# Products of a constant on the unread PSUM columns of two delta-rule scans

## The chip, the cores and the metric

The kernel runs on one core of one Trainium2 chip, as one launch. The metric is the device time of that launch in microseconds. The kernel before took 4370.02 us, the median of three runs (4360.15 to 4377.07 us). One further execution was profiled; all views of the profile below are of it.

The names used for the engines are those of the profile: PE is TensorE (PEld its weight loads), DVE is VectorE, ACT is ScalarE, POOL is GpSimd, SP is SyncE.

## The reference, cut to what matters

The program is a network of eight stages (L0_attn, L0_ffn, L1_attn, L1_ffn, L2_attn, L2_ffn, L3_attn, L3_ffn) over an input of 8 sequences x 512 tokens x 128 features, in float32. The change touches two of them, L0_attn and L2_attn. Each holds a delta rule: a state matrix per head is corrected token by token, and each token reads it. In L2_attn it is gated:

```
def step(S, inp):
    q_t, k_t, v_t, g_t, b_t = inp
    S = S * jnp.exp(g_t)[..., None, None]
    kv = jnp.einsum('bhk,bhkv->bhv', k_t, S)
    delta = (v_t - kv) * b_t[..., None]
    S = S + k_t[..., :, None] * delta[..., None, :]
    o = jnp.einsum('bhk,bhkv->bhv', q_t, S)
    return (S, o)
```

L0_attn has the same rule without the decay, written over chunks of 32 tokens. Both have 4 heads with keys of 32; the values are 32 wide in L0_attn and 64 wide in L2_attn, so a state row over all heads has W = 128 columns in L0_attn and W = 256 in L2_attn.

## The kernel before

The kernel goes through the stages one after the other. Tokens lie on the 128 partitions; a sequence is 4 tiles of 128 tokens (TPB = 4).

**How a delta rule is computed.** The kernel takes a chunk of 128 tokens at a time. Inside a chunk the token-by-token recurrence becomes a triangular system, whose inverse is built ahead of the scan for all 16 (head, chunk) pairs of a sequence by `inverse_steps` (L1244): blocks of 32x32 first, by doubling, with 64 products of 32x32 for each half step (L1275 `px`, L1282 `pz`), then blocks of 64 (L1294 to L1328). `pair_scores` (L1376) makes the token-by-token products `ps_a` (L1387). The scan itself, `scan_steps` (L1331), then goes through the four chunks in order. For a chunk c it issues on PE

- `pk` (L1344): the keys times the state S, W columns; DVE adds it to the values (`dr`, L1346). Not for c = 0, where the state is zero;
- `pd` (L1351): four products, one for each head, of the inverse with `dr` (with the values for c = 0), dv columns each; ACT copies the result out (`dd`, L1353);
- `pS` (L1357): the keys times `dd`, W columns, the update of the state; DVE masks it (`dS`, L1359), then POOL (L1362) or DVE (L1364) adds the old state. Not for c = 3;
- `po` (L1365): the queries times the state (L1367) and four products with `dd` (L1370), the output, which the stage's own `out` takes from PSUM (L481 in L0_attn, L1562 in L2_attn).

That is 3 + 4 + 4 + 3 = 14 PSUM tiles for a sequence. Each tile is a whole bank, 128 x 512 float32, of which only the first W columns are written and read. They come from the ring `psD`, which has two banks in both stages (L263, L1403); `single` (L814) hands out the next one of the ring.

**What sets the order of the work around the scan.** Both stages run several sequences at different phases at once. `together` (L1608) takes generators and advances the one that is furthest behind its share of steps, so that scan steps of one sequence stand between inverse steps of the next, preparation of the one after, and output work of the one before (L267 to L277 in L0_attn, L1425 to L1432 in L2_attn). On top of that the tile framework places each engine's instructions itself when the program is built, so instructions that depend on nothing yet may come to stand elsewhere than in the text. Once built, each engine runs its list in order, and waits on semaphores of the others.

**Number formats.** All of the products named above have float32 operands. A product with float32 operands appears in the trace as two pairs of weight load and matmul; one with bfloat16 operands as one pair. L2_attn already has one product in bfloat16 for each chunk, which adds a mask by way of an identity: L1522, `pdec<-cm,id`, 512 columns, its moving operand repeated over the heads by a broadcast (`bc`, L22).

Of the kernel before, what the change touches and what calls it, by code (L numbers as in the profile page):

```python
# [10 lines left out]
BF16 = mybir.dt.bfloat16  # L11
# [4 lines left out]
P = 128  # L16
# [5 lines left out]
def bc(ap, axis, n):  # L22
    a = ap.unsqueeze(axis)
    shape = list(a.shape)
    shape[axis] = n
    return a.to_broadcast(shape)


class Net:
# [186 lines left out]
    def L0_attn(self):  # L216

        nc, tc, T, NB, NT = self.nc, self.tc, self.T, self.NB, self.NT  # L220
        H, E, NL = 4, 32, 2
        with ExitStack() as es:
            cp = es.enter_context(tc.tile_pool(name="a0", reuse_waits="tile", side="right", bufs=1))
            w = {k: self.load(cp, f"L0_attn_{k}_proj_w", [D, D]) for k in ("q", "k", "v", "o")}
            cw = {k: self.load(cp, f"L0_attn_{k}_conv_w", [D, 4]) for k in ("q", "k", "v")}
            w["b"] = self.load(cp, "L0_attn_b_proj_w", [D, H])
            fs = self.load(cp, "L0_attn_fir_short_w", [D, 5])
            bones = self.load(cp, "c_hmask32", [P, H])
            bd = self.load(cp, "c_bmask32", [P, P])
            hT = cp.tile([D, NB, L], F32, name="hT")  # L230

            vt = cp.tile([P, TPB + 1, NB, D], F32, name="vt")
            nc.gpsimd.memset(vt[:, 0], 0.0)
            ls = cp.tile([P, NB, TPB, D], F32, name="ls")
            ll = cp.tile([P, NT, D], F32, name="ll")
            gc = es.enter_context(tc.tile_pool(name="a0g", reuse_waits="tile", side="right", bufs=1))
            lp = es.enter_context(tc.tile_pool(name="a0l", reuse_waits="tile", bufs=1))
            self.inverse_buffers(gc, 1)
            f = {"w1a": self.load(gc, "fw1a", [D, D], src=T["L0_attn_fuse_w1"][:D, :])}

            f["w1b"] = gc.tile([P, D], F32, name="w1b")
            nc.vector.memset(f["w1b"], 0.0)
            for h in range(H):
                nc.sync.dma_start(f["w1b"][h * 32 : h * 32 + 16, :], T["L0_attn_fuse_w1"][D:, :])
            f["st"] = gc.tile([P, TPB, H, 32], F32, name="st")
            nc.gpsimd.memset(f["st"], 0.0)
            f["b1"] = self.load(gc, "L0_attn_fuse_b1", [D, 1])
            f["w2"] = gc.tile([D, 32], F32, name="w2")
            nc.gpsimd.memset(f["w2"], 0.0)
            nc.sync.dma_start(f["w2"][:, :4], T["L0_attn_fuse_w2"])  # L250
            f["b2"] = self.load_row(gc, "L0_attn_fuse_b2", 4)
            f["onw"] = self.load(gc, "L0_attn_o_norm_w", [D, 1])
            f["rs"] = [self.load_row(gc, f"L0_attn_res_scale_{k}", 1) for k in ("short", "long")]
            lt = self.load_row(gc, "L0_attn_logit_temp", 1)
            tm = gc.tile([P, 1], F32, name="tm")
            self.softplus(tm, lt, gc, [P, 1])
            nc.vector.tensor_scalar(tm, tm, 1e-4, None, ALU.add)
            nc.vector.reciprocal(tm, tm)
            f["tm"] = tm
            st = [{"b": b, "hT": hT[:, b, :], "vt": vt[:, 1:, b, :], "ls": ls[:, b], "ll": ll[:, b * TPB : (b + 1) * TPB, :]} for b in range(NB)]  # L260
            self.ps = es.enter_context(tc.tile_pool(name="ps", reuse_waits="tile", bufs=1, space=bass.MemoryType.PSUM))
            last = es.enter_context(tc.tile_pool(name="psl", reuse_waits="tile", side="right", bufs=1, space=bass.MemoryType.PSUM))
            self.rings = {"psA": 1, "psC": 1, "psD": 2, "psF": (2, last)}  # L263
            for b in range(NB):
                self.L0_values(hT[:, b, :], vt[:, 1:, b, :], ls[:, b], w["v"], cw["v"], fs, lp, b)
            fir = self.L0_fir(vt, ll, lp)
            for n in range(-1, NB + 2):  # L267
                part = lambda m, g, k, late=0.0: (g(st[m]), k, late) if 0 <= m < NB else None
                self.together(
                    part(n, lambda s: self.inverse_steps(s["NT"], lp, "psC"), 15),  # L270
                    part(n - 1, lambda s: self.L0_scan(s, bd, lp), 12),
                    part(n - 2, lambda s: self.L0_fuse(s, f, w["o"], lp), 14),
                    part(n + 1, lambda s: self.L0_prep(s, w, cw, bones, lp), 11),
                    (fir, 16) if n == -1 else None,

                    *((self.L0_route(b, lp), 4, b * 0.1) for b in range(NB - 1) if n == NB + 1),
                )  # L277
            for _ in self.L0_route(NB - 1, lp):
                pass
# [964 lines left out]
    def inverse_steps(self, NT, pool, tag):  # L1244
# [77 lines left out]
        for u in range(2):  # L1322
# [5 lines left out]
            nc.vector.tensor_copy(nt[:64, gs, 64:], grp(pz[:64, :], 64))  # L1328
            yield

    def scan_steps(self, dv, kbT, qT, NT, AT, vb, kt, bd, out, pool, tag, ac=None):  # L1331

        nc = self.nc
        H = 4
        W = H * dv
        S = None
        for c in range(TPB):
            cs = slice(c * P, (c + 1) * P)  # L1340
            r = vb[:, c, :]
            if S is not None:
                pk = self.single(tag, "pk")
                nc.tensor.matmul(pk[:, :W], kbT[:, cs], S, start=True, stop=True)  # L1344
                r = pool.tile([P, W], F32, tag="dr", name="dr", bufs=1)
                nc.vector.tensor_tensor(r, vb[:, c, :], pk[:, :W], ALU.add)  # L1346
                yield
            pd = self.single(tag, "pd")
            for h in range(H):
                hs = slice(h * dv, (h + 1) * dv)  # L1350
                nc.tensor.matmul(pd[:, hs], NT[:, h, c, :], r[:, hs], start=True, stop=True)  # L1351
            dl = pool.tile([P, W], F32, tag="dd", name="dd", bufs=2)
            nc.scalar.copy(dl, pd[:, :W])  # L1353
            yield
            if c < TPB - 1:
                pS = self.single(tag, "pS")
                nc.tensor.matmul(pS[:, :W], kt[:, c, :], dl, start=True, stop=True)  # L1357
                Sn = pool.tile([P, W], F32, tag="dS", name="dS", bufs=2)
                nc.vector.tensor_tensor(Sn, pS[:, :W], bd, ALU.mult)  # L1359
                if S is not None:  # L1360
                    if ac is None:
                        nc.gpsimd.tensor_tensor(Sn, Sn, S, ALU.add)  # L1362
                    else:
                        nc.vector.scalar_tensor_tensor(Sn, S, ac[:, c : c + 1], Sn, ALU.mult, ALU.add)  # L1364
            po = self.single(tag, "po")  # L1365
            if S is not None:
                nc.tensor.matmul(po[:, :W], qT[:, cs], S, start=True, stop=False)  # L1367
            for h in range(H):
                hs = slice(h * dv, (h + 1) * dv)
                nc.tensor.matmul(po[:, hs], AT[:, h, c, :], dl[:, hs], start=S is None, stop=S is None or h == H - 1)  # L1370
            out(c, po[:, :W])
            if c < TPB - 1:
                S = Sn
            yield
# [17 lines left out]
    def L2_attn(self):  # L1392
# [3 lines left out]
        nc, tc, T, NB = self.nc, self.tc, self.T, self.NB  # L1396
        H, V = 4, 64
        with ExitStack() as es:
            cp = es.enter_context(tc.tile_pool(name="a2", reuse_waits="tile", side="right", bufs=1))
# [16 lines left out]
            for k, src in (("id", "ident"), ("cm", "c_cmaskT")):  # L1416
                f = self.ident if src == "ident" else self.load(cp, src, [P, P])
                c[k] = cp.tile([P, P], BF16, name=f"{k}16")
                nc.vector.tensor_copy(c[k], f)
            na = cp.tile([P, H], F32, name="na")  # L1420
            nc.scalar.activation(na, row["A_log"], AF.Exp)
            nc.vector.tensor_scalar(na, na, -1.0, None, ALU.mult)
# [752 lines left out]
```

## Time and profile before

| | us |
|---|---|
| median of 3 runs | 4370.02 (4360.15 to 4377.07) |
| the profiled execution, its own time | 4375.92 |
| its span, first to last instruction | 4374.1 |
| PE busy in the span | 3713.5 (85%) |
| DVE busy | 2393.6 (55%) |
| ACT busy | 1691.1 (39%) |
| POOL busy | 1575.7 (36%) |
| mean granted TensorE clock | 0.822 of full speed |

The profiled execution took 5.9 us more than the median of the runs; 1.8 us of its time lie outside its span.

How to read it: "busy" is the time in which at least one instruction of the engine is under way. PE's instructions overlap, so a busy PE need not be a PE at its peak. The granted clock is that of TensorE alone, as a share of its full speed; the profile has it for each piece of the span. The scans run from 211 to about 740 us (L0_attn) and from 2449 to 2988 us (L2_attn).

### The profile page before, as it was taken

What the parts mean: (1) busy time and instruction counts of PE and PEld (TensorE: products, weight loads), DVE (VectorE), ACT (ScalarE), POOL (GpSimd) and SP (SyncE); (2) the same over time, 40 slices, a digit from 0 to 9 for tenths busy, and PEclk for the clock granted to TensorE, in tenths of its full rate; (3) what the DMA queues carried; (4) which work ended last, traced back from release to release, by engine and by line L of the source; (5) the groups of instructions that cost most, each with busy time, mean ns of one, the idle gap of its engine ahead of it and who ended that gap; (6) DMA issues with size and microseconds to landing.
All of it is one profiled execution on the core that took longest, in us unless ns stands there. A gap on an engine that the chain in (4) does not pass through costs nothing.

```text
span 4374.1 us, 101816 instructions
## 1 busy us (share of the span) xinstructions
PE 3713.5 (85%) x44392; PEld 2680.3 (61%) x44456; DVE 2393.6 (55%) x5943; ACT 1691.1 (39%) x2545; POOL 1575.7 (36%) x1557
## 2 busy tenths in 40 slices
PE   5999998648999999897376999996999899986998
PEld 3777786545655656554254777774666566655666
DVE  6446565335454454554627566534777776655333
ACT  3224333113444444443024445422556566631221
POOL 1212221462111111222274343423455555423775
PEclk6566656678999999997586778766999999997998
DMA  2200000240200000000140000001000000002554
GB/s 66 60 3 2 3 7 14 82 127 1 82 7 2 4 7 1 4 1 20 29 84 13 3 3 3 2 3 41 1 1 1 1 1 7 1 8 72 149 147 126
DMA packets 125917, 130.60 MB, mean 30 GB/s; under 512 B 18496, under 2 KB 107280, under 8 KB 125472
## 3 DMA queue, kind: packets, MB, share of 16 engines
q0 software_dynamic: 30816, 67.62, 5.9%
q1 hardware_dynamic: 94656, 56.47, 4.5%
q8 instruction: 349, 5.72, 0.5%
q14 instruction: 96, 0.79, 0.1%
HBM read 96.85 MB, written 27.20 MB: 28 GB/s over the span
## 4 chain that ended last, share of the span: by engine, by line
PE 44%; DVE 16%; ACT 7%; POOL 5%; DMA 4%; issue 3%; POOLq 0%; another core or an unknown queue 0%; DVEq 0%; ACTq 0%; SPq 0%
PE ps_h L1023 4%; PE po L1029 3%; DMA acc<-y,tl_idx 2%; PE ps_qk L1721 2%; PE ps_s L897 2%; POOL nm_r L70 2%; DVE nm_st L65 2%; DVE mt L906 2%; PE ps_a L1387 1%; PE ps_tr L825 1%; PE ps_s L975 1%; PE pav L965 1%; PE po L1837 1%; PE pg L1984 1%; POOL r L1751 1%
## 5 line engine op out<-in xcount | busy, mean ns | idle before, releaser
L70 POOL TENSOR_TENSOR nm_r<-nm_r,mhalf 128x4 f32<-128x4 f32 x168 | 173.3, 1032 | 448.9 <-DVE nm_r L69 430.7
L1733 POOL TENSOR_TENSOR r<-r,rot 128x512 f32<-128x512 f32 x128 | 162.8, 1272 | 305.3 <-DVE rot L1732 249.4
L1030 DVE TENSOR_TENSOR y<-y,po 128x512 f32<-128x512 f32 x32 | 22.0, 687 | 307.9 <-PE po L1029 307.9
L928 POOL TENSOR_TENSOR cn<-cx,rc 64x448 f32<-64x448 f32 x32 | 37.5, 1173 | 413.5 <-DVE rc L926 413.5
L1023 PE MATMUL ps_h<-hTm,w 128*128 128x512 f32 x256 | 162.0, 718 | 11.2 <-ACT hid L1024 4.8
L979 ACT ACTIVATE pT<-ps_s 128x2048 f32<-128x2048 f32 x64 | 106.5, 1664 | 167.7 <-PE ps_s L977 167.7
L1721 PE MATMUL ps_qk<-wqkv,hTq 128*128 128x512 f32 x256 | 148.1, 674 | 18.3 <-DVE hTq L1713 6.1
L1271 POOL TENSOR_TENSOR iM<-iN,c_lvl 128x512 f32<-128x512 f32 x64 | 86.7, 1365 | 183.2 <-PE px L1275 167.1
L975 PE MATMUL ps_s<-qa,kT 32*128 32x256 f32 (+1 forms) x1024 | 149.7, 405 | 0.6 <-DVE mt L906 0.3
L624 POOL DMA_INDIRECT xr<-rows_in,tl_idx x124 | 118.8, 958 | 71.4 <-PE pt L671 17.5
L621 POOL DMA_INDIRECT acc<-y,tl_idx x78 | 124.8, 1600 | 45.1 <-DVE y L1994 21.7
L1024 ACT ACTIVATE hid<-ps_h,b 128x512 f32<-128x512 f32 x128 | 87.9, 687 | 130.7 <-PE ps_h L1023 129.6
L1029 PEld LDWEIGHTS po<-w,hid 128*128 128x128 f32 x1024 | 121.7, 198 | 20.9 <-ACT hid L1024 20.9
L1029 PE MATMUL po<-w,hid 128*128 128x128 f32 x1024 | 127.8, 285 | 5.8 <-ACT hid L1024 1.6
L1751 POOL TENSOR_TENSOR r<-r,rn 128x512 f32<-128x512 f32 x128 | 129.0, 1041 | 1.9
L1282 PEld LDWEIGHTS pz<-iTT,iX 32*32 32x32 f32 x8192 | 92.5, 120 | 51.4 <-issue 33.7
L1282 PE MATMUL pz<-iTT,iX 32*32 32x32 f32 x8192 | 103.7, 208 | 23.3 <-issue 16.5
L1723 ACT ACTIVATE sq<-ps_qk 128x512 f32<-128x512 f32 x128 | 75.8, 592 | 122.1 <-PE ps_qk L1721 122.0
L1275 PEld LDWEIGHTS px<-iT,iM 32*32 32x32 f32 x8192 | 96.8, 125 | 41.3 <-issue 27.3
L906 DVE TENSOR_REDUCE mt<-ps_s 128x8 f32<-128x2048 f32 x32 | 73.4, 2292 | 87.2 <-PE ps_s L899 87.2
L1275 PE MATMUL px<-iT,iM 32*32 32x32 f32 x8192 | 107.5, 213 | 10.6 <-issue 9.3
L1789 DVE TENSOR_REDUCE mx<-ps_s 128x8 f32<-128x1024 f32 x64 | 77.8, 1216 | 61.9 <-PE ps_s L1786 61.9
(681 smaller groups left out, 10626.8 us busy)
## 6 DMA issues: line engine op xcount, KB each, us to landing
fcur<-in_L_attn_fir_cur SPq DMA_DIRECT2D x32, 256.0 KB, 2.8
acc<-z SPq DMA_DIRECT2D x16, 512.0 KB, 6.9
sum<-acc SPq DMA_DIRECT2D x32, 256.0 KB, 3.0
rows_out<-y SPq DMA_DIRECT2D x23, 128.0 KB, 2.9
x<-in_L_attn_hidden_states SPq DMA_DIRECT2D x8, 256.0 KB, 4.8
fprev<-in_L_attn_fir_prev SPq DMA_DIRECT2D x8, 256.0 KB, 3.6
rows_in<-rx SPq DMA_DIRECT2D x8, 256.0 KB, 2.3
w<-in_L_attn_W SPq DMA_DIRECT2D x8, 256.0 KB, 2.8
```

Of the source, the lines that this page charges most:

```text
L70: nc.gpsimd.tensor_tensor(r, r, self.mhalf[:, :G], ALU.pow)
L621: self.nc.gpsimd.indirect_dma_start(out=dst, out_offset=bass.IndirectOffsetOnAxis(ap=idx, axis=0), in_=src, in_offset=None, compute_op=ALU ...
L624: self.nc.gpsimd.indirect_dma_start(out=dst, out_offset=None, in_=src, in_offset=bass.IndirectOffsetOnAxis(ap=idx, axis=0))
L906: nc.vector.tensor_reduce(m4, s4, AX.X, ALU.max, negate=True)
L975: nc.tensor.matmul(ss[:, h, n * 256 : n * 256 + W], kT[R[h], k * P : (k + 1) * P], qa[R[h], k * P : k * P + W], start=True, stop=False)
L1023: nc.tensor.matmul(ps, self.cols(w["w1"], f), hT, start=True, stop=True)
L1029: nc.tensor.matmul(self.cols(po, t), self.cols(hid[:, f, :], t), w["w2"][:, f, :], start=(f == 0), stop=(f == FC - 1))
L1275: nc.tensor.matmul(px[p, g * B : (g + 1) * B], nm[p, g, :], Ti[p, g, :], start=True, stop=True)
L1282: nc.tensor.matmul(pz[p, g * B : (g + 1) * B], X[p, g, :], TT[p, g, :], start=True, stop=True)
L1721: nc.tensor.matmul(ps, self.cols(hT, t), w["qkv"][:, j, :], start=True, stop=True)
L1733: nc.gpsimd.tensor_tensor(r3, r3, m, ALU.add)
L1751: nc.gpsimd.tensor_tensor(r3, r3, bc(rn[:, j, t, :], 2, E), ALU.mult)
```

## The change

A constant `fill`, the identity in bfloat16, is made in each of the two stages. Each of the 14 PSUM tiles of a scan is now taken through a new function `busy`. It takes the bank from the ring as before, and then issues two products of `fill` with `fill` (repeated over the columns by a broadcast) into the columns W to 511 of that bank, which nobody reads: 384 columns in L0_attn, 256 in L2_attn. The scan's own products follow into the first W columns.

```
@@ L0_attn and L2_attn, each
+            self.fill = cp.tile([P, P], BF16, name="fill")
+            nc.vector.tensor_copy(self.fill, self.ident)
@@ new, ahead of scan_steps
+    def busy(self, tag, name, used):
+
+
+        ps = self.single(tag, name)
+        for _ in range(2):
+            self.nc.tensor.matmul(ps[:, used:], self.fill, bc(self.fill, 1, (512 - used) // P), start=True, stop=True)
+        return ps
+
@@ scan_steps
-                pk = self.single(tag, "pk")
+                pk = self.busy(tag, "pk", W)
...
-            pd = self.single(tag, "pd")
+            pd = self.busy(tag, "pd", W)
...
-                pS = self.single(tag, "pS")
+                pS = self.busy(tag, "pS", W)
...
-            po = self.single(tag, "po")
+            po = self.busy(tag, "po", W)
```

## The prediction

> **What bounds the kernel now.** I first read the page's slices of the span, each 109 us long: how busy PE is, and which TensorE clock was granted.
>
> ```profile
> PE   5999998648999999897376999996999899986998
> ...
> PEclk6566656678999999997586778766999999997998
> ```
>
> In both stages of the change (slices 2 to 7 and 23 to 27 of 40) PE is nearly always busy, yet its clock stands at 5 or 6 tenths in the first and 6 to 8 in the second, against 9 in most slices of the other stages. The view by stretches puts numbers on the two scans:
>
> ```profile
> core 0: us, PE busy (x) PEld busy (x) DVE busy (x) ACT busy (x) POOL busy (x), PEclk, DMA share, GB/s
> 200.00:745.00 545.00, 507.58 (x10352) 416.58 (x10351) 308.27 (x625) 191.71 (x313) 123.72 (x135) 0.60 0.02 5
> 2448.00:2985.00 537.00, 496.75 (x10483) 407.71 (x10481) 295.57 (x628) 228.90 (x350) 184.01 (x179) 0.75 0.01 3
> ```
>
> PE is busy for 93% of each stretch, DVE, the next, for 57% and 55%. So PE sets the end of both, and what a product costs there depends on the clock. The clock's own records hold two values alone, 0.5 and 1.0, for pieces that are multiples of 3.413 us; a mean of 0.60 is 33 such windows of 160 at full clock, 0.75 is 80 of 157. What opens it? I asked for single windows, cut where the records cut.
>
> ```profile
> 423.22:426.63 3.41, 3.41 (x136) 3.35 (x133) 0.48 (x2) 3.38 (x7) 1.27 (x1) 0.50 0.02 5
> 426.63:430.05 3.42, 3.42 (x135) 3.13 (x136) 2.75 (x10) 1.84 (x3) 0.00 (x0) 0.50 0.02 5
> ...
> 2539.47:2542.88 3.41, 3.41 (x10) 1.92 (x8) 0.42 (x1) 1.65 (x3) 1.27 (x1) 0.50 0.02 5
> 2542.88:2546.29 3.41, 3.41 (x141) 2.77 (x141) 1.26 (x2) 0.57 (x2) 0.00 (x0) 1.00 0.02 5
> ```
>
> The first three are all wholly busy at half clock; only after the third does the clock open. They differ in what the timeline of PE shows in them:
>
> ```profile
> 423.06 1.93 PE L1275 MATMUL px<-iT,iM 32*32 32x32 f32 x128
> 424.92 0.80 PE L1357 MATMUL pS<-dd,kt 128*128 128x128 f32 x2
> 425.51 1.75 PE L1370 MATMUL po<-dd,AT 128*128 128x32 f32 x8
> ...
> 2539.43 1.21 PE L1344 MATMUL pk<-dS,kbT 128*128 128x256 f32 x2
> 2540.44 0.63 PE L1522 MATMUL pdec<-cm,id 128*128 128x512 bf16 x1
> 2540.87 1.91 PE L1521 MATMUL pdec<-gm,c_gt 128*128 128x512 f32 x2
> ```
>
> So I counted columns. A column that streams past a full 128x128 float32 stationary counts 1, one past a smaller stationary a quarter, one of a bfloat16 product a half; an instruction is spread evenly over its duration. The first window holds about 1024 (128 x 32 / 4) + 256 (2 x 128) + 150 = 1430, the third about 510 + 256 + 1024 + 140 = 1930. Counted so over all 1275 windows of the trace, the next window is at full clock after 5 of the 444 below 1500, after 9 of the 26 from 1500 to 1550, and after 804 of the 805 above, whichever clock they had themselves. I take 1547 as the mark, where a fit puts it. The quarter is fitted too (0.25). The half is the weak weight: few windows at the mark hold bfloat16, and 0.45 to 0.8 fit about equally well; 0.3 misjudges 28 windows in place of 12.
>
> The Trainium skill, "TensorE: Matmul & The Clock Gate", section "Why this matters for your kernels", speaks against the change: it asks only that TensorE be kept busy for 4 us or more and have no idle gaps. By it, windows like the first two, PE busy without a gap, should be at full clock already, and more work could only cost; the sum would be that of the slower rival below. The windows decide against the rule here: busy at 0.50 is their usual state.
>
> **The change, part by part.** Each sequence takes 14 banks through `busy`, with two products each: 14 x 2 x 8 = 224 in each stage, as many matmuls and weight loads as the built program shows more on PE. Nothing is removed. One DVE cast a stage (the like of L1419, 0.22 us) falls into the stages' preparation, where DVE is about half idle; uncovered it is 0.4 us in all.
>
> *Price of one product.* L1522 is the same form: bfloat16, an identity, 512 columns, broadcast. Its durations contain latency, so I take end to end. At half clock it ends 2540.44 + 0.63 = 2541.07, L1344 ahead of it 2540.64: 0.43 us (0.426 in the records' nanoseconds). At full clock:
>
> ```profile
> 2461.95 0.70 PE L1344 MATMUL pk<-dS,kbT 128*128 128x256 f32 x2
> 2462.48 0.38 PE L1522 MATMUL pdec<-cm,id 128*128 128x512 bf16 x1
> ```
>
> 2462.86 - 2462.65 = 0.21 (0.216). Scaled by columns, 384 cost 0.320 or 0.162 us, 256 cost 0.213 or 0.108. They lie on the path: PE's idle time is 7% of the stretches, and mostly elsewhere.
>
> *Weight loads.* The first product of a scan tile ended 0.51 us after a 32x32 product (L1357 after L1275, half clock, median of 7) but 0.21 us after a full-array one: its load had been exposed by 0.30 (0.20 at full clock). About 100 of the 224 tiles come after a small product. A fill in between hides that load in the two thirds of tiles where the built order leaves it directly ahead, and exposes its own load (0.15 or 0.10, L1522's): 100 x (2/3 x 0.25 - 0.125) = 4 us gained, 2 a stage.
>
> *Waits.* A fill waits for the bank, as the tile's first product did. Its former reader (L1346, L1353, L1359 or `out`) always stands before the operand that the product itself waits for, so I price this at nothing; uncovered, 50 to 100 tiles by a DVE read of about 0.3 us (L1346, 0.42 in L2_attn) are 15 to 30 us. Behind a held fill on PE stand the inverse's products (L1275, L1282), and their readers L1277 on ACT and L1283 on DVE would be late next. The built order also moves other PE instructions, by up to 268 places of 25573; no row prices that, and I bound it by 15 us either way.
>
> *Clock, L0_attn.* Fills add 2 x 384 / 2 = 384 to the count for a tile, and push out work of the half-clock window that they lengthen (0.64 of 3.41 us). Of 119 windows below the mark at half clock, 11 then reach it, 26 if nothing is pushed out. A full-clock run lasted 3.3 windows (33 in 10 runs), and one in five of its windows would have been at full clock anyway: 1 + 2.3 x 0.79 = 2.8 new windows for each, 31, and two more where a run is kept alive: 33 new. What is one worth? Eight weight-bound products took 1.75 at half clock (L1370 above) and 0.98 at full (L1351 at 450.72 us of the timeline), wide ones gain 0.426 / 0.216, so 1.9 for four fifths of the time; 128 of 32x32 gain 1.93 / 1.35 = 1.43 for the fifth that L1275 and L1282 take; and 6% of the full-clock windows is idle on issue. Together 0.94 / (0.8 / 1.9 + 0.2 / 1.43) = 1.68: a new window does 0.68 x 3.41 = 2.3 us more. Gain 33 x 2.3 = 76. Cost at the new mix (66 of 160 at full clock): 224 x 0.75 x (0.59 x 0.426 + 0.41 x 0.216) = 57, less 2. **L0_attn: 21 us less.** With 11 new windows it is 35 us more, with 26 x 2.8 = 73 some 120 less.
>
> *Clock, L2_attn.* 256 more for a tile: 9 windows reach the mark (17 if nothing is pushed out). Six are the last or next to last of a cold stretch and bring one window each; three stand together in the long cold stretch from 2885 to 2946 us, where the last scan runs almost alone, and bring about seven. 13 x 2.3 = 30. Cost at 93 of 157: 224 x 0.5 x (0.41 x 0.426 + 0.59 x 0.216) = 34, less 2. **L2_attn: 2 us more.** Bounds: 6 new windows, 20 more; 26, 30 less.
>
> *Sum.* 4375.9 - 21 + 2 = 4357 for an execution like the profiled one, which was 5.9 us over the median: **4351 us**, 0.43% below it. The likeliest case's own range is 4320 to 4380.
>
> **The rivals.**
> *Slower: the gate does not pay.* The cost is sure, the gain is not. If these products hardly count (an identity times an identity is nearly all zeros; L1522, the nearest row, has an identity on one side only), or only push counted work out of the window, the clock stays as it is and 224 x 0.75 x 0.382 = 64 and 224 x 0.5 x 0.319 = 36 us come on top, less 4: 4466. It decides from fewer than about (55 + 34) / 2.3 = 39 new windows in both stages; I count 46, which is close. Halfway, with 25, it is some 4405. For it: 0.45 is within the weight's bounds, and 15 of the 26 windows need work not to be pushed out. Against it: bfloat16 windows in the trace do count.
> *Much faster: L0_attn keeps itself open.* Its full-clock windows held 1797 on average, above the mark, and half-clock windows 960, which at 1.68 times the pace is 1613. Near the mark, 384 more could hold long runs: 73 new windows, 4250 to 4300. Against it: the count varies, and one poor window closes the gate.
> *Order or banks:* a fill ahead of a bank not yet free holds PE, 15 to 30 us: 4385 to 4400. Against it: the readers' order above.
> That the products are not made is excluded by the built program.
>
> **How the numbers follow.** About 0.5% is what a measurement of this kernel can tell from no change, here 22 us: below 4348, above 4392. Chances: forecast 0.48, gate does not pay (fully or halfway) 0.32, much faster 0.14, order or banks 0.06. The forecast lies near the bound: half of it is faster, nearly half within. Faster 0.25 + 0.14 = 0.39; slower: of the rivals' 0.38 some 0.29 lie above 4392; within 0.5%: 0.32. The range reaches into both sides: 4285 to 4430.
>
> **What would show it.** PE's row for `fill` at about 0.32 or 0.16 us a product end to end; the clock of the L0_attn stretch near 0.70 in place of 0.60, of L2_attn near 0.80; L0_attn shorter by some 20 us, L2_attn unchanged; stretches outside unchanged. If L0_attn's clock stays below 0.65 the gate rival holds; if the clock rises and the time doesn't fall, another engine or the new order took it, which the waits before the `fill` products and PE's idle time would show.

## The result and the profile after

The changed kernel took 4387.02 us, the median of 20 runs (4369.13 to 4409.66), against 4374.9 us for the kernel before in 20 runs beside it (4360.15 to 4389.57). The medians are 12 us apart; the ratio over all the runs is 1.0036 with a 95% interval of 1.0022 to 1.0049, which is about 16 us. The change made the kernel slower, by less than the 0.5% that was called "no change", where 4351 us, a gain, had been forecast. The profiled execution has a span of 4378.9 us and a mean granted clock of 0.837.

First the slices of the changed kernel's page, each 109 us long: how busy PE is, in tenths, and the granted clock, in tenths of full speed.

```profile
PE   5989998649999999897377999986899899986998
...
PEclk6576767779999999996576778676999999997998
```

In slices 3 to 7, L0_attn's, the clock has risen, from 5 and 6 tenths to 6 and 7. In slices 24 to 28, L2_attn's, hardly a digit has moved. The stretches of the same bounds as before say it in numbers (columns: the bounds, the length, busy time of PE, PEld, DVE, ACT and POOL with their instructions, granted clock, DMA share, GB/s):

```profile
200.00:745.00 545.00, 492.13 (x10605) 398.29 (x10603) 316.12 (x636) 190.79 (x315) 118.33 (x135) 0.70 0.02 6
2448.00:2985.00 537.00, 494.84 (x10199) 405.22 (x10198) 300.85 (x609) 226.09 (x342) 177.95 (x176) 0.75 0.01 3
```

L0_attn went from 0.60 to 0.70, as forecast; L2_attn stayed at 0.75, where 0.80 had been forecast. In L0_attn PE is also busy for 15 us less of the 545.

All the new products stand on one line, L1338. The view of that line (smallest, median and largest duration in ns):

```profile
L1338 PE MATMUL pd<-fill x128: 269/326/528, 87.5 to 2995.1; 128*128 128x384 bf16 x64, 128*128 128x256 bf16 x64
L1338 PE MATMUL po<-fill x128: 272/326/528, 217.4 to 2996.6; 128*128 128x384 bf16 x64, 128*128 128x256 bf16 x64
L1338 PE MATMUL pS<-fill x96: 272/327/528, 88.1 to 2991.7; 128*128 128x384 bf16 x48, 128*128 128x256 bf16 x48
L1338 PE MATMUL pk<-fill x96: 272/332/528, 221.6 to 2994.4; 128*128 128x384 bf16 x48, 128*128 128x256 bf16 x48
```

128 + 128 + 96 + 96 = 448 products, 224 in each stage: the change does what it says. These durations hold latency; the price shows end to end. The timeline of PE at two places of L0_attn, one at half clock, one at full:

```profile
425.73 1.75 PE L1380 MATMUL po<-dd,AT 128*128 128x32 f32 x8
427.29 0.83 PE L1338 MATMUL pk<-fill 128*128 128x384 bf16 x2
427.91 0.64 PE L1354 MATMUL pk<-dS,kbT 128*128 128x128 f32 x2
...
503.79 0.97 PE L1380 MATMUL po<-dd,AT 128*128 128x32 f32 x8
504.60 0.49 PE L1338 MATMUL pk<-fill 128*128 128x384 bf16 x2
504.93 0.38 PE L1354 MATMUL pk<-dS,kbT 128*128 128x128 f32 x2
```

At half clock two fills end at 428.12, the products ahead of them at 427.48: 0.32 us each. At full clock 505.09 - 504.76 = 0.33 for two, 0.165 each. The forecast had 0.320 and 0.162. The scan's own product behind them, one float32 product that the trace shows as two matmuls, ends 0.43 and 0.22 us later. That is 0.21 or 0.11 us for each matmul, with no exposed load in front.

A reading by stage, from one profiled execution of each kernel, stands ahead of the runs, since each of them is read with it. "L0_attn" is the time at which that stage ends; "L2_attn" is the length of that stage with its projections; "full" is the time at full clock in each, in L0_attn from the first record of the clock on, some 20 us into the span. One execution of a stage is not exact. In L0_attn `before` and `l2_only` have the same order of instructions on PE, and so have `after` and `l0_only`; they differ by 8 and 7 us. In L2_attn six kernels have one order, on all engines (`before`, `l0_only`, `l0_four` and those with one, six and eight products further down), and their lengths go from 669.2 to 694.6 us.

```
kernel         ratio of runs [95%]         L0_attn  full   L2_attn  full
before         1                           791.6    146.8  692.9    327.7
after          1.0036 [1.0022, 1.0049]     784.0    262.8  715.3    337.9
l0_only        0.9992 [0.9969, 1.0016]     790.7    266.2  691.1    337.9
l2_only        1.0045 [1.0026, 1.0064]     783.6    163.8  714.4    341.3
tiny           1.0101 [1.0065, 1.0137]     799.7    146.8  718.7    317.4
quarter        1.0279 [1.0246, 1.0313]     864.5    139.9  745.6    317.4
l0_four        0.9891 [0.9853, 0.9930]     742.9    375.5  669.2    341.3
inverse        1.0140 [1.0109, 1.0171]     808.1    256.0  731.2    337.9
l0_spread      0.9971 [0.9947, 0.9995]     772.5    406.2  673.6    344.7
both_spread    1.0007 [0.9979, 1.0034]     769.8    395.9  681.4    484.7
```

### The profile page after: what moved, and what is told of

Its sections match the earlier page's. It is cut to its first block, busy times and chain, and to the rows that moved or that the text cites. A ratio compares the mean times of both kernels' runs of the same rounds, so it can differ in the third digit from the quotient of the medians.

```text
span 4378.9 us, 102777 instructions
## 1 busy us (share of the span) xinstructions
PE 3712.1 (85%) x44904; PEld 2667.2 (61%) x44904; DVE 2411.6 (55%) x5945; ACT 1688.7 (39%) x2543; POOL 1570.1 (36%) x1557
## 4 chain that ended last, share of the span: by engine, by line
PE 42%; DVE 17%; ACT 7%; POOL 5%; DMA 4%; issue 2%; POOLq 0%; DVEq 0%; ACTq 0%
PE ps_h L1025 4%; PE po L1031 3%; DMA acc<-y,tl_idx 3%; POOL nm_r L70 2%; PE ps_qk L1733 2%; DVE nm_st L65 2%; PE ps_s L899 2%; DVE mt L908 2%; PE ps_s L977 1%; PE ps_a L1397 1%; POOL r L1763 1%; PE pav L967 1%; PE po L1849 1%; PE pg L1996 1%; PE ps_tr L827 1%
```

## The experiments

All kernels are edits of the changed kernel. None leaves out a part of the computation: what they alter is written only into columns that nobody reads, or that are overwritten before they are read.

**The two stages apart.** The products in L0_attn alone (`l0_only`), and in L2_attn alone (`l2_only`).

```
 l0_only
-        for _ in range(2):
+        for _ in range(2 if used == P else 0):
 l2_only
-        for _ in range(2):
+        for _ in range(0 if used == P else 2):
```

> The products in L0_attn alone (L2_attn takes its banks plainly). Theory A, clock against price: in each stage the change is worth the new full-clock windows at about 2.3 us each less the price of the products; the profile after has 31 new windows in L0_attn (8 us shorter) and 5 in L2_attn (22 us longer). So here L0_attn keeps the clock 0.70 of its scan stretch and ends about 8 us earlier than in the kernel before, L2_attn is as before (693 us, clock 0.75), and the time is 5 to 15 us below that of the kernel before. Theory B, order: the added instructions change the built order and this alone moves the time; then the stage without products can move too, and nothing ties the gain to the clock.

> The products in L2_attn alone. Theory A: the scan's tiles lie mostly in windows that are at full clock already, so few new windows (about 5) against some 32 us of price: L2_attn 15 to 25 us longer than before, its scan clock still 0.75 to 0.77, L0_attn as before; the time 15 to 25 us above the kernel before. Theory B: any sign.

Measured: 4363.58 us, ratio 0.9992 [0.9969, 1.0016], and 4387.56 us, ratio 1.0045 [1.0026, 1.0064]. The loss is L2_attn's. By the runs `l2_only` is 11 to 28 us slower than the kernel before, some 20 us; by the profiles L2_attn has 714.4 and 715.3 us with the products, 692.9 and 691.1 without, 23 us more, and above all six lengths of the order without them. `l0_only` lies between 14 us faster and 7 us slower than the kernel before, so the 21 us forecast for L0_attn did not come. By the profiles that stage has 787.4 us on average with its products (784.0, 790.7) and 787.6 without (791.6, 783.6): 25 to 31 more full-clock windows and nothing to show for them.

**The same products, counted less.** `tiny` makes products of 32 columns in place of 384 or 256; `quarter` keeps the columns and the durations, but uses 32 of the 128 rows, so that by the count a column is worth a quarter.

```
 tiny
-            self.nc.tensor.matmul(ps[:, used:], self.fill, bc(self.fill, 1, (512 - used) // P), start=True, stop=True)
+            self.nc.tensor.matmul(ps[:, 480:], self.fill, self.fill[:, :32], start=True, stop=True)
 quarter
+            self.nc.tensor.matmul(ps[:, used:], self.fill[:32, :], bc(self.fill[:32, :], 1, (512 - used) // P), start=True, stop=True)
```

> All 448 products stay, in the same banks and with the same waits, but write 32 columns each (480 to 511) in place of 384 or 256. They hardly stream and hardly count. Theory A: both clocks as before (0.60 and 0.75); the gain of L0_attn is gone, the loss of L2_attn too: each stage between unchanged and 8 us longer (two weight loads a tile, partly against the exposed load that a product hides). Theory B (order, waits for banks, weight loads hidden): the same as with the change, L0_attn about 8 us shorter and L2_attn about 22 us longer, though the clock hasn't moved.

> Same products, same columns, same banks, but only 32 of the 128 rows of the constant are used, so each streams as long and counts a quarter by the count of columns. Theory A: the price is paid and the clock hardly gained: L0_attn's scan clock 0.60 to 0.65 in place of 0.70, L2_attn's 0.75 or less, 30 to 60 us longer in L0_attn and 20 to 40 in L2_attn, 60 to 100 us above the kernel before in all. Theory B, or a gate that only asks whether PE is busy: as with the change, about 12 us above.

Measured: `tiny` 4411.57 us, 1.0101 [1.0065, 1.0137]; `quarter` 4493.17 us, 1.0279 [1.0246, 1.0313]. The two stretches of `quarter`, in the columns used above:

```profile
200.00:815.00 615.00, 589.70 (x10562) 443.47 (x10560) 309.61 (x620) 187.78 (x310) 115.17 (x133) 0.59 0.02 5
2515.00:3110.00 595.00, 563.51 (x10717) 427.33 (x10716) 307.07 (x629) 229.84 (x351) 185.28 (x179) 0.73 0.01 4
```

PE is busy for 96% of the first stretch, more than in any other kernel here, and its clock is 0.59. In both stages the built order is that of the changed kernel, instruction for instruction, so in L0_attn the same order, with products that stream as many columns past a quarter of the rows, stays at the 0.59 or 0.60 of the kernel without products: what opened the clock after the change was the count, not the order of PE's instructions and not its busy time. The Trainium skill's advice to keep TensorE busy for 4 us or more ("TensorE: Matmul & The Clock Gate", section "Why this matters for your kernels") does not agree with these rows.

The price of `quarter` is not a clean one, though. Its timeline beside the groups shown of the changed kernel:

```profile
457.89 2.05 PE L1380 MATMUL po<-dd,AT 128*128 128x32 f32 x8
459.87 0.81 PE L1338 MATMUL pk<-fill 32*128 32x384 bf16 x2
460.62 0.80 PE L1354 MATMUL pk<-dS,kbT 128*128 128x128 f32 x2
```

The two fills end at 460.68, 0.74 us after the products ahead in place of 0.64, and the scan's product at 461.42, another 0.74 us later in place of 0.43. Weight loads that lay hidden beside a full-array product come out beside one of 32 rows: 0.1 us in front and 0.3 us behind. The trace shows it: in the changed kernel the load for the scan's product starts 0.32 us before the product, at 427.59 us, while a fill still runs; here it starts together with the product, at 460.62. The same in `tiny`:

```profile
449.77 0.66 PE L1277 MATMUL px<-iT,iM 32*32 32x32 f32 x31
450.36 0.24 PE L1338 MATMUL pk<-fill 128*128 128x32 bf16 x2
450.44 0.78 PE L1354 MATMUL pk<-dS,kbT 128*128 128x128 f32 x2
```

The fills end 0.17 us after the 32x32 products, and the scan's product 0.62 us after the fills in place of 0.43: a product of 32 columns is over before the next load is in. So `tiny` bears a price of its own, and its 26 us more in L2_attn do not measure the order alone. Nor is its order the changed kernel's: in L0_attn it lies much nearer to that of the kernel before. What it does say is that its own order, with almost free products, gains nothing.

**More products in L0_attn.** Since two bring windows but no time there, one, three, four, six and eight a tile.

```
-        for _ in range(2):
+        for _ in range(4 if used == P else 0):
```

(and 1, 3, 6 and 8 in place of 4.)

> The products in L0_attn's scan tiles alone, four for each tile in place of two: 448 of 384 columns. Theory A as the prediction had it (a new full-clock window is worth 2.3 us, a product costs its own 0.32 or 0.16 us): some 54 new windows against 90 us of products, L0_attn 30 to 40 us shorter than before. Theory C (the same windows, but a product in a full-clock window costs 1.66 times its duration, since that is the pace of the work it pushes out: 1.53 against 0.92 us of half-clock work for each us, as the traces of before and after have it): the gain is eaten, L0_attn within 15 us of before although its clock rises above 0.70.

> One product a tile in L0_attn's scan. Theory G: full-clock time 190 to 220 us (before 147 to 164, two 266), gain and price even, the kernel within 12 us of before. Theory E: set by the wait before the score tiles.

> L0_attn's scan tiles alone, three products a tile (two: within 10 us of before; four: 58 below). Theory G, dose: what the products open grows faster than what they cost until most of the stretch is at full clock, so three lie between: full-clock time in L0_attn 300 to 340 us (two 266, four 375), the kernel 20 to 45 us below before. Theory E, order: the build with two products makes PE wait 10 to 12 us for DVE before the score tiles (ps_a, DVE NT), the one with four does not, and it is this that makes the step; then three follows its own wait: near two if the wait is there, near four if not.

> Six products a tile in L0_attn's scan. Theory G: full-clock time 400 to 450 us, some 60 more, worth 40 us, against some 224 more products of which most are at full clock and cost 0.27 us of work each: 60; the kernel 10 to 25 us slower than with four, still 25 to 50 below before. Theory E: set by the wait before the score tiles.

> Eight products a tile in L0_attn's scan. Theory G: the clock hardly rises further (430 to 470 us at full), the price does: about as before, within 25 us. Theory E: set by the wait before the score tiles.

Measured, with the stretch from 200 us to the last scan product of the stage, from one profile each; "wait" is PE's idle time before `ps_a` for DVE (`NT` or `AT`, L1389 before the change and L1399 after it):

```
products  ratio [95%]               stretch  full clock  PE idle  wait
0 (before)                          540.7    112.6       36.6     0.8
1         0.9981 [0.9959, 1.0004]   522.5    219.0       57.6     4.9
2         0.9992 [0.9969, 1.0016]   542.8    219.0       48.5     9.7
3         0.9991 [0.9971, 1.0012]   534.6    273.1       48.5     11.5
4         0.9891 [0.9853, 0.9930]   492.1    321.2       29.8     0.7
6         0.9918 [0.9891, 0.9944]   503.5    387.3       32.8     1.5
8         0.9991 [0.9964, 1.0019]   536.8    423.3       30.2     0.3
```

The profiled executions lie 14 us below the kernel's median with one product, 7 below with three, 24 below with six and 12 above with eight, so the stretches are to be read with that in mind. Time at full clock grows with the products, but for one and two, which have the same; the kernel's time does not follow. Four take 4318.63 us against 4376.36 us before (medians; by the ratio 48 us less), and six gain 0.8%; eight hold full clock for 79% of the stretch and are no faster than none. Neither price in the expectation of four held: a product at its own duration was to leave L0_attn 30 to 40 us shorter than before, a product at 1.66 times that in full-clock windows within 15 us; it was 49 us shorter (742.9 against 791.6). Nor does one of the later theories sort the kernels alone. By dose three should have gained 20 to 45 us. By the wait, three is where it should be, with two; but eight has no wait and gains nothing. The stretch of `l0_four`, and the slices of its clock:

```profile
200.00:692.00 492.00, 462.24 (x10759) 361.59 (x10758) 305.29 (x619) 184.51 (x307) 125.45 (x134) 0.83 0.02 6
```

```profile
PEclk6687986869999999998576787867999999997998
```

The clock is 0.83 there and PE is busy for 94%, where the changed kernel has 90%. Two things can be read from the groups and waits of the changed kernel's stretch, 200 to 745 us, and of this one. First the 64x64 products and the waiting `ps_a` of the kernel before, 200 to 800 us (line, operands, shapes, count, busy us, mean ns of one, idle before):

```profile
L1327 PE MATMUL pz<-NT,iX 64*64 64x64 f32 x256 | 32.8, 316 | 1.6 <-DVE NT L1328 1.6
L1387 PE MATMUL ps_a<-kbT,kT 32*128 32x128 f32 x192 | 23.8, 360 | 2.3 <-issue 0.8 <-DVE NT L1389 0.8 <-ACT kbT L827 0.7
```

Of the changed kernel:

```profile
L1277 PE MATMUL px<-iT,iM 32*32 32x32 f32 x3584 | 48.9, 219 | 6.1 <-issue 5.3 <-DVE iT L1287 0.7
L1329 PE MATMUL pz<-NT,iX 64*64 64x64 f32 x256 | 32.7, 315 | 2.2 <-DVE NT L1330 1.6 <-ACT iX L1322 0.7
L1397 PE MATMUL ps_a<-fq,kT 32*128 32x128 f32 x208 | 30.1, 439 | 3.0 <-DVE NT L1399 3.0
L1397 PE MATMUL ps_a<-kbT,kT 32*128 32x128 f32 x192 | 17.2, 325 | 9.0 <-DVE NT L1399 8.9
```

And of the kernel with four products:

```profile
L1277 PE MATMUL px<-iT,iM 32*32 32x32 f32 x3584 | 40.8, 200 | 3.2 <-DVE iT L1287 1.8 <-issue 1.1 <-PE ph L356 0.2
L1329 PE MATMUL pz<-NT,iX 64*64 64x64 f32 x256 | 25.1, 268 | 1.8 <-ACT iX L1322 1.0 <-DVE NT L1330 0.8
L1397 PE MATMUL ps_a<-fq,kT 32*128 32x128 f32 x208 | 22.2, 348 | 0.0
L1397 PE MATMUL ps_a<-kbT,kT 32*128 32x128 f32 x192 | 16.8, 312 | 2.1 <-issue 1.4 <-DVE NT L1399 0.7
```

With two products the 64x64 products still take 315 ns on average, as before the change (316): none of them had come into a full-clock window. With four they take 268, and the scores `ps_a` 348 in place of 439. And the wait of `ps_a` for `NT`, 0.8 us in all before the change, 11.9 us after it, is 0.7 us again.

Where does that wait come from? `quarter`, whose order in L0_attn is the changed kernel's, has 2.8 us of it at low clock; the changed kernel and `l0_only` have 11.9 and 9.7 us. So in that order it is longer where PE runs faster. In the order built with four products it is gone although PE runs faster still. Order and pace both have a part; no run separates them.

**Other places.** Products ahead of the inverse's tiles `px` and `pz` in place of the scan's (`inverse`: as many, as long, 448), and one product of 512 columns ahead of every tile that `single` hands out, in L0_attn (`l0_spread`, 382 products) or in both stages (`both_spread`, 806). The scan's own are left out in all three, and `self.spread` is the width, zero outside the stages.

```
+        ps = pool.tile([P, 512], F32, tag=tag, name=name, bufs=n)
+        if self.spread and (name in ('px', 'pz')):
+            for _ in range(2):
+                self.nc.tensor.matmul(ps[:, : self.spread], self.fill, bc(self.fill, 1, self.spread // P), start=True, stop=True)
+        return ps
 l0_spread and both_spread: one product a tile, whatever its name
```

> The same number of products of the same widths (224 of 384 columns in L0_attn, 224 of 256 in L2_attn), taken out of the scan's tiles and put ahead of the 14 tiles px and pz of each inverse, where the later products write over them. Theory A and C: the place decides. Counted over the windows of the trace before, 7 windows of L0_attn (11 with the scan's tiles) and 6 of L2_attn (9) reach the mark, and each product after a 32x32 product exposes a load (0.11 us): L0_attn 10 to 30 us longer than before, L2_attn 15 to 40 us longer, clocks 0.63 to 0.70 and 0.74 to 0.78. Theory D (any even mixing of such work opens the gate, place is no matter): as with the change.

> L0_attn alone: one product of 512 columns ahead of every PSUM tile that the stage takes through the common function (382 in all: inverse, preparation, scan, output), none in L2_attn. Theory C: spread evenly, 256 of the count for a tile and about 2.4 tiles a window lift most windows over the mark; with the clock at 0.9 of full L0_attn is 20 to 45 us shorter than before, with 0.8 about 10 shorter. If the 32x32 products' exposed loads (0.11 to 0.14 us each side) weigh more, no gain.

> As l0_spread, and the same in L2_attn (424 more products of 512 columns). Theory C for L2_attn: half of its windows are at full clock without help, so half of the products are pure price at 1.66 times 0.216 us; the cold stretches hold 300 to 1400 of the count and open only partly: L2_attn 10 to 60 us longer than before.

Measured: `inverse` 4439.6 us, 1.0140 [1.0109, 1.0171]; `l0_spread` 4362.21 us, 0.9971 [0.9947, 0.9995]; `both_spread` 4376.1 us, 1.0007 [0.9979, 1.0034]. In `inverse` L0_attn had 256 us at full clock, about what the changed kernel has, and was 16 us longer than before all the same. The view of its fill line says what held PE:

```profile
L825 PE MATMUL px<-fill x224: 269/372/528, 6.5 to 3023.1; 128*128 128x384 bf16 x56, 128*128 128x256 bf16 x56
L825 PE MATMUL pz<-fill x224: 269/332/528, 156.0 to 3032.5; 128*128 128x384 bf16 x56, 128*128 128x256 bf16 x56
its engine sat idle before it (us, times) until:
...
  DVE NT L1319: 39.6, 25
```

Here the fills do wait, 40 us in all, for the bank behind `NT`: the mechanism of the third rival, at a place where the reader of a bank comes late. At the scan's tiles no fill waits on another engine. `both_spread` opened the clock widest, here its two stages:

```profile
200.00:737.00 537.00, 492.23 (x10690) 362.20 (x10688) 313.45 (x646) 190.79 (x315) 118.60 (x134) 0.79 0.02 6
2437.00:2998.00 561.00, 514.51 (x10924) 394.08 (x10924) 311.93 (x655) 238.47 (x363) 189.49 (x185) 0.89 0.03 11
```

0.89 in L2_attn, 140 us more at full clock than in `l0_spread`, which has the same products in L0_attn and none there. Yet by one profile of each the stage is 8 us longer than in that kernel (681.4 against 673.6), well within the spread above: what the clock gave, the products took. In the two kernels L0_attn is 15 and 18 us shorter than the average without products; `l0_spread` gains 13 us by the runs, with an interval that just leaves out 1, and `both_spread` nothing at its median. The profiled execution of `both_spread` is 12 us shorter than that of the kernel before: 22 us less in L0_attn, 11 less in L2_attn, and 21 more in the rest of the kernel, 2911 us against 2890. The rest has 2905 to 2911 us in all four kernels that ran on this chip (`l0_four`, `inverse` and the two of this kind) and 2876 to 2891 in all the others, so profiles of different chips are best compared by whole kernels, each against the kernel before beside it.

## Why the prediction failed

The forecast was a gain of 19 us on a median of 4370.0 us; the median of the kernel before in 20 runs is 4374.9, so 5 of the 36 us by which 4351 missed lie in the base. The rest splits about evenly, by the runs of each stage alone: `l0_only` gained some 3 us where 21 were forecast, `l2_only` lost some 20 where 2 were.

**What held.** The price of a product, the load that a fill hides, the count that opens the gate, and the windows that it opens in L0_attn. The same count that was fitted on the kernel before sorts the changed kernel's windows: with a weight of 0.55 for bfloat16, about 10 of some 1270 are misjudged, with 0.3 over 25, and with nothing for the fills about 50. An identity times an identity counts like any other product, against the doubt in the first rival. In the stretch of L0_attn 31 windows are new, 219.7 us at full clock against 112.6, where the forecast had 33 (25 against `l2_only`, whose L0_attn has no products either and 133.1 us).

**The step that failed in L0_attn: "Cost at the new mix".** It charged a product in a full-clock window its own duration, 0.162 us. But the gate opens windows of a fixed length. What a product takes there is time for work at the fast pace, and that work is then done elsewhere, at the slow one. To size the paces I gave each of the other products its mean end-to-end time at half clock, and divided the sum by the time in windows of each clock, fills left out. In L0_attn before the change that is 0.92 us of work per us at half clock and 1.53 at full. A new window is then worth (1.53 / 0.92 - 1) x 3.413 = 2.26 us, the forecast's 2.3; but each us of fill in a full-clock window costs 1.53 / 0.92 = 1.66 us. The fills of the changed kernel take 25.3 us at half and 26.3 us at full clock there. So the cost is 25.3 + 1.66 x 26.3 = 69, and not 51.6, and the 31 windows bring 70. The same as one balance: the stretch holds 567 us of work; 219.7 - 26.3 = 193.4 us at pace 1.53 do 296 of it, the other 271 take 295 us at 0.92, and with 25.3 us of fills and the 219.7 the stretch lasts 540 us. Before it lasted 540.7; measured after, 537.1 and 542.8. This price is worked out from the traces by one way of counting; no run measured it by itself, and the balance fits two products but not four, as said below. So that the sum left out the work which a fill pushes out of a full-clock window follows from windows of fixed length; that this is all that ate the gain is argued, not shown.

**In L2_attn two terms failed.** "13 x 2.3 = 30" was the first: the stretch has 85 full-clock windows against 81, four new ones and not 13. Even these may be none: `l0_only`, without products there, has 85 too, and over the stage the same 337.9 us at full clock as the changed kernel. The windows that were named as near the mark stayed shut because the products do not fall there. The middle of L2_attn in the kernel before, and its end, where the long cold stretch was to bring seven:

```profile
2560.00:2680.00 120.00, 112.82 (x2062) 92.83 (x2066) 77.88 (x173) 61.89 (x94) 53.71 (x54) 0.74 0.01 2
2680.00:2800.00 120.00, 111.46 (x2719) 88.89 (x2710) 76.10 (x169) 60.13 (x93) 46.05 (x47) 0.83 0.01 3
...
2885.00:2946.00 61.00, 55.57 (x1257) 47.59 (x1255) 21.95 (x33) 14.62 (x23) 15.69 (x14) 0.56 0.01 3
2946.00:2988.00 42.00, 35.97 (x272) 30.34 (x272) 12.12 (x31) 6.12 (x11) 3.54 (x3) 0.60 0.04 11
```

And in the changed kernel:

```profile
2560.00:2680.00 120.00, 113.62 (x1964) 94.96 (x1965) 76.94 (x164) 54.90 (x83) 46.29 (x49) 0.71 0.01 2
2680.00:2800.00 120.00, 112.68 (x2532) 88.59 (x2532) 77.96 (x162) 56.19 (x84) 41.78 (x43) 0.81 0.01 3
...
2880.00:2922.00 42.00, 38.76 (x478) 32.90 (x479) 17.75 (x32) 9.07 (x15) 12.98 (x14) 0.54 0.01 2
2922.00:2998.00 76.00, 65.55 (x1359) 54.35 (x1358) 24.25 (x53) 17.04 (x28) 10.69 (x10) 0.76 0.03 7
```

Only the very end opened, from 0.60 to 0.76. The 42 us from 2880 us on are as cold as ever, and hold eight of the stage's 224 products. Over the whole stretch 47 of the 79 half-clock windows hold no fill at all, while full-clock windows get more of their count from fills (217 of it on average) than half-clock ones (151). In the middle the clock even fell a little, to 0.71 and 0.81, from 0.74 and 0.83 in the same bounds before.

The second term is the price again: 21.0 us of fills at half and 17.7 us at full clock cost 21.0 + 1.66 x 17.7 = 50, with 38.7 in the forecast's manner of counting. Four windows would bring 9, so 41 us would be lost. 17 of them did not appear: the pace at half clock was 0.96 in place of 0.90. It did so in `quarter` as well (0.95), whose products are as long, and less in `tiny` (0.92), so part of the products' time lies over time that PE would have lost anyway; which loads or waits these are is open. What remains is 24 us, and 23 were measured in the profiles, some 20 in the runs.

**The rivals.** The first, that the gate does not pay, was to decide below 39 new windows; 31 + 4 = 35 came, so its halfway case (4405 us) is near, for another reason than given: the products count in full, but in L2_attn stand in the wrong windows. The second, L0_attn keeping itself open, did not happen with two products. It did with four, 321 of 492 us at full clock, and was worth 48 us by the ratio and not the 120 forecast. The third, "order or banks", had the range in which the result lies, 4385 to 4400 us, but by luck: no fill of the scan waits for its bank, and the loss stands in L2_attn. In another form it is there: PE's idle time in L0_attn rose from 36.6 to 49.1 us, of which 11 us are the wait of `ps_a` for `NT`. The pace at full clock, idle time included, was no lower (1.55, and 1.50 in `l0_only`), so the balance closes without blaming these 12 us. But they are most of the 18 us by which L0_attn fell short, the gain came with four products where they are gone, and no run separates them from the price.

**What stays open.** The balance at unchanged paces gives 540 us for four products too, as for two; measured were 492.1. Their paces were 0.96 at half and 1.66 at full clock: with these, which are read from the same trace and so explain nothing by themselves, the balance gives (567 - 1.66 x 259.1) / 0.96 + 33.3 + 321.2 = 497. The groups above show two parts of it, work that gains more from the clock (64x64 products ran 1.7 times as fast at full clock, 32x32 products 1.4 times) and 19 us less idle. Why three products have hardly any of it and four have both stays open; every number of products is another built order. So does the spread of L2_attn, 25 us in one and the same order.

## What to carry to other kernels

Work that is added to open a clock gate pays only in the windows that it opens. In a window already open it pushes out work that is then done at the slow pace, by the balance above 1.66 times its own duration (not measured by itself). So count where the fills fall, window by window, before counting what they open. Ask too which work stands in the new windows, since the pace gained differs by shape. And where a scheduler places instructions, try several amounts: here one, two and three products a tile could not be told from none, four gained 1.1%, six 0.8% and eight nothing. And compare whole kernels over many runs: the length of a stage in one profile moved by up to 25 us with nothing changed in it.

## What the hardware showed that was not expected

- TensorE can be busy for 96% of 615 us and be granted half clock for most of it (0.59, `quarter`); by the count, rows of the array in use and columns decide, not busy time.
- A product of 32 rows takes as long as one of 128 (0.320 us for 384 columns at half clock, one fill after another), but bares the loads beside it: 0.1 us before and 0.3 us after it at half clock. A bfloat16 product of 32 columns costs 27 ns alone at half clock, and leaves 187 ns of the next float32 load exposed.
- Full clock for longer is not less time: 423 us of it in a stretch of 537 (eight products) against 321 in 492 (four).
- The same order of instructions on all four engines took 669.2 to 694.6 us in L2_attn, in six profiled kernels on several chips, with 320.9 to 341.3 us at full clock.
